# Graph-attention sums of a two-layer GNN kernel: three single-pass products in place of full-precision products

## Chip, cores and metric

The kernel runs on one core of one Trainium2 chip, in one launch. The metric is the device time of that launch in microseconds (us). Engines are named as in the profile: PE (TensorE matmuls), PEld (its weight loads), DVE (VectorE), ACT (ScalarE), POOL (GpSimd), SP (SyncE, which here only issues DMAs).

## Reference

x has 1250 nodes with 1024 features, and there are 41250 edges. Cut to what matters (normalisation and the first layer are only named):

```
edge_index = jnp.stack([src, dst])
h = jnp.maximum(_layernorm(x), 0.0)
x = x + first_layer(h, ...)              # relational convolution, ELU, product with wo; residual h
h = jnp.maximum(_layernorm(x), 0.0)
# second layer: graph attention
h = h @ W                                # 1024 x 1024
al, ar = h @ a_l, h @ a_r
e = exp(-leaky_relu(al[src] + ar[dst], negative_slope=0.1))
rowsum = segment_sum(e, src, num_segments=N)
h_prime = segment_sum(e[:, None] * h[dst], src, num_segments=N)
x = x + elu(h_prime / (rowsum[:, None] + 1e-5))
```

The last segment sum is done densely: the weight of a pair of nodes is (number of edges between them) times e, and h_prime is the 1250 x 1250 weight matrix times h. All of it is float32.

## The kernel before

The 1250 nodes are T = 10 row tiles of 128 (the last has 98 rows). The program goes through four stages.

1. To about 190 us: edges are counted into `cnt` by one-hot products, and the first layer's three products with the weights are made (L720, float32).
2. To about 300 us: `means` (L791) multiplies the counts with y in three bfloat16 parts, `way_back` (L837, L838) multiplies with wo, `add_back` (L843) adds the result to the tile of x, which stays in on-chip memory to the end. The matmul at L838 is the only one in the single-pass 4-byte type `F32R`.
3. From 300 to about 439 us: h @ W. Tiles 0 and 1 are made by `product`. The other eight are made in pairs of tiles, each pair in two units (i, j) of seven half-size products (`p1` to `p7`, all through `seventh`, L946). ACT copies products out of PSUM, DVE adds others to them. `by_dst` (L1006) adds the counts of the two edge types and has a DMA transpose them. `scores` and `row` spread the attention scores for use by `weights`. The order inside this stage is left to the scheduler.
4. From 439 us to the end: for each row tile s, `weights(s)` makes the 128 x 1280 weights (L1017 score sums, L1019 leaky ReLU, L1021 masking by counts, L1022 exponential, L1023 times counts), and `sums(s)` multiplies them with all ten tiles of h (L1070): ten times three matmuls of 342 columns in float32. A column of ones in h gives the row sum. `finish` does the division, the ELU and the residual: DVE at L1034 and L1040, ACT at L1035 and L1038, POOL at L1039 (adds the tile of x), then one DMA of the tile to the output. The last tile goes through `finish_last` in three narrower blocks. weights(s+1) is made while the products of s run.

`long_tile`, `new_h`, `turned` and the `yh`, `x`, `w` tags are the places in on-chip memory which tiles share one after another. Inside `tc.manual_schedule` PE, DVE and ACT keep the order in which the program is written; each engine runs its own instructions in order everywhere.

Of the kernel before, what the change touches and what calls it, by code (L numbers as in the profile page):

```python
# [410 lines left out]
def fast_arm(tc, ctx, edges, firsts, w_root, conv_bias, wo, w_gat, a_gat, out,  # L411
             ident, eps5, eps6, lnw, const, wt, wcat, bias, xs, cnt_raw,
# [8 lines left out]
    FB = [(0, 128), (128, 256)]  # L421
    cnt = cnt_raw.rearrange("p (h r n) -> p h r n", h=T, r=2)
# [15 lines left out]
    def norm_relu(work, xt, n):  # L438
# [11 lines left out]
        h = work.tile([128, D], F32, name="h")  # L450
# [20 lines left out]
    with ExitStack() as c1:  # L471
        hot = c1.enter_context(tc.tile_pool(name="hot", bufs=5))

        room = [yh.tile([128, F + 3 * (F + 2)], F32, name=f"room{t}", tag=f"yh{t}") for t in (9, 8, 7)]
# [113 lines left out]
        def first_part(t):  # L588
# [3 lines left out]
            y = yh.tile([128, F + 3 * (F + 2)], F32, name=f"y{t}", tag=f"yh{t}")  # L592
# [141 lines left out]

    def long_tile(name):
        return work.tile([128, T * 128], F32, name=name, tag="z", bufs=2)
# [8 lines left out]
    rest_w = work.tile([128, D], F32, name="rest_w", tag="h")  # L745
# [22 lines left out]
    wo4 = work.tile([128, D], F32R, name="wo4")  # L768
# [72 lines left out]
    def add_back(t, po):  # L841
        n = ROWS[t]
        nc.vector.tensor_add(xs[t][:n], xs[t][:n], po[:n].rearrange("p a b -> p (a b)"))  # L843

# [12 lines left out]
    def new_h(t):  # L857
        hg = yh.tile([128, D + 2], F32, name=f"h{t}", tag=f"yh{t}")
        hs[t] = hg
        return hg.rearrange("p (h c) -> p h c", h=2)  # L860

    def scores(t):

        n = ROWS[t]
        ends = hs[t].rearrange("p (h c) -> p h c", h=2)[:n, :, H]
        nc.vector.tensor_copy(score[:n, :, t], ends)
        nc.gpsimd.memset(hs[t][:n, H:H + 1], 1.0)
# [17 lines left out]
    slots = [cnt[:, s, 0, :D + 2].bitcast(F32) for s in range(T)] + [meta[:, :H + 1], meta[:, H + 1:D + 2]]  # L885
    t1s, t2s, t4s = slots[0:4], slots[4:8], slots[8:12]
# [46 lines left out]
    def rest_of_pair(i):  # L933
# [3 lines left out]
        p["s4"] = s4  # L937
# [65 lines left out]
    def by_dst(s):  # L1003

        tot = cnt[:, s, 0, :]
        nc.vector.tensor_tensor(tot, tot, cnt[:, s, 1, :], ALU.add)  # L1006
        nc.sync.dma_start_transpose(cnt[:, s, 1, :].rearrange("p (t n) -> p t n", t=T), tot)

    zs = {}

    def weights(s, t0, t1):

        if s not in zs:
            zs[s] = long_tile("z").rearrange("p (t n) -> p t n", t=T)
        c = cnt[:, s, 1, :].rearrange("p (t n) -> p t n", t=T)[:, t0:t1]
        z = zs[s][:, t0:t1, :]
        nc.vector.tensor_tensor(z, rows[:, s:s + 1, :].to_broadcast([128, t1 - t0, 128]),  # L1017
                                n_ar[:, t0:t1, None].to_broadcast([128, t1 - t0, 128]), ALU.add)
        nc.vector.scalar_tensor_tensor(z, z, 0.1, z, op0=ALU.mult, op1=ALU.min)  # L1019

        nc.vector.scalar_tensor_tensor(z, c, 1e30, z, op0=ALU.mult, op1=ALU.min)  # L1021
        nc.scalar.activation(z, z, AF.Exp)  # L1022
        nc.vector.tensor_mul(z, c, z)  # L1023

    def finish(s, inv, parts):

        n = ROWS[s]
        low, high = wt[s % 2], wt[2 + s % 2]
        for p, c0, c1 in parts:
            shape = dict(a=p.shape[1]) if len(p.shape) == 3 else None  # L1030
            lo, hi = low[:n, c0:c1], high[:n, c0:c1]
            if shape:
                lo, hi = (v.rearrange("p (a b) -> p a b", **shape) for v in (lo, hi))
            nc.vector.tensor_scalar(lo, p, inv[:n], 0.0, op0=ALU.mult, op1=ALU.min)  # L1034
            nc.scalar.activation(hi, p, AF.Relu, scale=inv[:n])  # L1035
        lo, hi = low[:n, :D + 1], high[:n, :D + 1]
        low, high = (v[:n].rearrange("p (h c) -> p h c", h=2)[:, :, :H] for v in (low, high))
        nc.scalar.activation(lo, lo, AF.Exp)  # L1038
        nc.gpsimd.tensor_add(high, high, xs[s][:n].rearrange("p (h c) -> p h c", h=2))  # L1039
        nc.vector.scalar_tensor_tensor(lo, lo, -1.0, hi, op0=ALU.add, op1=ALU.add)  # L1040
        nc.sync.dma_start(out[s * 128:s * 128 + n, :].rearrange("p (h c) -> p h c", h=2), low)

    def finish_last(s, inv, p, h0, h1, c0, c1):

        n = ROWS[s]
        lo, hi, x = (w[:n].rearrange("p (h c) -> p h c", h=2)[:, h0:h1, c0:c1]
                     for w in (wt[s % 2], wt[2 + s % 2], xs[s]))
        nc.vector.tensor_scalar(hi, p, inv[:n], 0.0, op0=ALU.mult, op1=ALU.max)
        nc.scalar.activation(lo, p, AF.Exp, scale=inv[:n])
        nc.vector.tensor_add(hi, hi, x)  # L1050
        nc.vector.scalar_tensor_tensor(lo, lo, 1.0, hi, op0=ALU.min, op1=ALU.add)
        nc.sync.dma_start(out[s * 128:s * 128 + n, :].rearrange("p (h c) -> p h c", h=2)[:, h0:h1, c0:c1], lo)

    def sums(s):
        n = ROWS[s]
        z = zs.pop(s)

        def inverse(rowsum):
            inv = small("inv")
            nc.vector.tensor_scalar_add(inv[:n], rowsum, 1e-5)  # L1060
            nc.vector.reciprocal(inv[:n], inv[:n])
            return inv

        if s < T - 1:
            pp, p3 = three("p3")
            for t in range(T):
                for i, (c0, c1) in enumerate(CUTS):
                    c1 = min(c1, D + 1)
                    o = pp[:n, i, :c1 - c0] if i < 2 else p3[:n, :c1 - c0]
                    nc.tensor.matmul(o, z[:ROWS[t], t, :n], hs[t][:ROWS[t], c0:c1], start=(t == 0),  # L1070
                                     stop=(t == T - 1))
            finish(s, inverse(pp[:n, 1, H - 342:H - 341]), [(pp[:n, :, :342], 0, 684), (p3[:n, :341], 684, D + 1)])
        else:

            nc.gpsimd.tensor_scalar_add(xs[s][:n], xs[s][:n], -1.0)
            QH = 448
            for i, (h0, h1, c0, c1) in enumerate([(1, 2, 0, QH), (0, 1, 0, QH), (0, 2, QH, H)]):
                p = bank("p3").rearrange("p a b -> p (a b)")
                o = p[:n, :QH + 1] if i == 0 else p[:n, :(h1 - h0) * (c1 - c0)]
                for t in range(T):  # L1080
                    h = hs[t][:ROWS[t]]
                    cols = h[:, H:H + 1 + QH] if i == 0 else h.rearrange("p (h c) -> p h c", h=2)[:, h0:h1, c0:c1]
                    nc.tensor.matmul(o, z[:ROWS[t], t, :n], cols, start=(t == 0), stop=(t == T - 1))  # L1083
                if i == 0:
                    inv = inverse(o[:, 0:1])
                    o = o[:, 1:]
                finish_last(s, inv, o.rearrange("p (h c) -> p h c", h=h1 - h0), h0, h1, c0, c1)
# [43 lines left out]
    with tc.issue_after(copied[T - 1]):  # L1131
        for s in range(T):
            by_dst(s)
# [5 lines left out]
    s12 = work.tile([128, 2, KH, 128], F32, name="s12", tag="wo4")  # L1139
# [186 lines left out]
```

## Time and profile before

| | us |
|---|---|
| median of 3 runs (620.19 to 620.54) | 620.24 |
| the profiled execution's own time | 620.34 |
| span of the profile, first to last instruction | 618.4 |
| PE busy | 607.4 (98%) |
| DVE busy | 379.6 (61%) |
| ACT busy | 191.0 (31%) |
| POOL busy | 45.1 (7%) |
| granted TensorE clock, mean | 0.996 |

The last stage takes 438.8 to 618.4 us of the span; in 438.8 to 611.0 us PE is busy without a gap, DVE for 100.75 us, ACT for 33.05 us and POOL for 23.47 us. In the lines of the profile L is the line of the kernel, "out<-in" names tiles, "128x512" is partitions times elements. In a timeline a line gives the start, the duration, the engine, the line and the tiles of one instruction (or of several alike, "x4"), and in brackets how long the engine sat idle before it and for what.

### The profile page before, as it was taken

To read this page: it belongs to the slowest core of one execution; us is meant where nothing else is said; L and a number is where in the kernel's file an instruction comes from. 1 tells how busy PE (TensorE), PEld (TensorE's weight loads), DVE (VectorE), ACT (ScalarE), POOL (GpSimd) and SP (SyncE) were. 2 spreads that over 40 slices of the span, in tenths; PEclk is the share of its full clock that TensorE was granted. 3 is DMA by queue.
4 is the path that set the end of the run, shared out by engine and by line. 5 is a ranking of instruction groups with operands and counts; after the bars stand their busy time and mean duration, and the time that the engine had idled before them with its cause. 6 is when DMAs were issued, how large, how long until landed. Compare 5 with 4: busy or idle time off the path is not lost.

```text
span 618.4 us, 7877 instructions
## 1 busy us (share of the span) xinstructions
PE 607.4 (98%) x2828; PEld 416.7 (67%) x2828; DVE 379.6 (61%) x899; ACT 191.0 (31%) x385; POOL 45.1 (7%) x56
## 2 busy tenths in 40 slices
PE   8999999999999999999999999999999999999995
PEld 5566666666657776777667888888666666666652
DVE  5889887787754846679974131233555555666632
ACT  3766556666532000014311223131112211222210
POOL 5010000000000000000000000010011101111110
PEclk9999999999999999999999999999999999999998
DMA  8950111111019200000470000000000000000001
GB/s 281 352 110 16 21 34 36 34 36 27 2 53 318 71 2 1 1 1 1 76 137 1 0 2 0 1 0 1 2 0 35 34 34 36 34 35 34 34 37 31
DMA packets 23688, 30.26 MB, mean 49 GB/s; under 512 B 14550, under 2 KB 14874, under 8 KB 23638
## 3 DMA queue, kind: packets, MB, share of 16 engines
q1 hardware_dynamic: 22070, 24.53, 12.7%
q0 software_dynamic: 1424, 5.12, 4.4%
q8 instruction: 24, 0.39, 0.3%
q14 instruction: 26, 0.21, 0.1%
q10 hardware_dynamic: 144, 0.00, 0.0%
HBM read 16.13 MB, written 5.12 MB: 34 GB/s over the span
## 4 chain that ended last, share of the span: by engine, by line
PE 95%; DMA 2%; SPq 1%; DVE 0%; ACT 0%; issue 0%
PE mm L720 18%; PE mm L1070 17%; PE mm L946 11%; PE mm L791 11%; PE p L1070 8%; PE acc L520 7%; PE mm L837 6%; PE z L946 4%; PE mm L875 3%; PE p L1083 3%; DMA w<-in_w_cat_dram 2%; PE p L875 1%; PE tp L575 1%; PE mm L838 1%; PE tp L910 1%; PE tp L926 1%
## 5 line engine op out<-in xcount | busy, mean ns | idle before, releaser
L720 PE MATMUL mm<-w,hT 128*128 128x429 f32 (+1 forms) x320 | 143.7, 535 | 1.4 <-DMA w<-in_w_cat_dram 1.4
L1070 PE MATMUL mm<-h,z 128*128 128x342 f32 (+1 forms) x360 | 118.5, 450 | 0.0
L519 DVE TENSOR_SCALAR key<-meta 125x320 bf16<-125x320 f16 x330 | 85.5, 301 | 24.2 <-PE acc L520 12.0
L1070 PEld LDWEIGHTS mm<-h,z 128*128 128x128 f32 (+1 forms) x360 | 68.4, 190 | 34.9
L791 PE MATMUL mm<-y,cnt 128*128 128x286 bf16 (+3 forms) x600 | 74.9, 284 | 0.2 <-DVE y L613 0.2
L520 PEld LDWEIGHTS <-lo 125*128 125x128 bf16 x330 | 40.5, 126 | 50.4 <-issue 37.2
L520 PE MATMUL acc<-key,lo 125*128 125x320 bf16 x330 | 72.2, 303 | 0.0
L527 ACT ACTIVATE cnt<-acc 128x320 f32 x110 | 49.9, 454 | 69.9 <-PE acc L520 61.4
L791 PEld LDWEIGHTS <-cnt 128*128 128x128 f16 (+1 forms) x600 | 59.3, 99 | 14.4 <-issue 0.8
L1070 PE MATMUL p<-h,z 128*128 128x341 f32 (+1 forms) x180 | 66.1, 449 | 0.0
L720 PEld LDWEIGHTS mm<-w,hT 128*128 128x128 f32 (+1 forms) x320 | 51.4, 191 | 6.7 <-issue 5.1
L1070 PEld LDWEIGHTS p<-h,z 128*128 128x128 f32 (+1 forms) x180 | 33.7, 188 | 17.7
L946 PE MATMUL mm<-w,a 128*128 128x257 f32 (+3 forms) x192 | 44.8, 380 | 0.0
L946 PEld LDWEIGHTS mm<-w,a 128*128 128x128 f32 (+1 forms) x192 | 35.6, 187 | 6.0 <-ACT h L972 0.4
L837 PE MATMUL mm<-wo,meta 128*128 128x512 f32 (+1 forms) x80 | 37.6, 592 | 0.0
L1039 POOL TENSOR_TENSOR w<-w,x 128x1024 f32<-128x1024 f32 x9 | 23.4, 2597 | 135.3 <-ACT w L1035 135.3
L1019 DVE SCALAR_TENSOR_TENSOR z<-z 128x1280 f32<-128x1280 f32 (+2 forms) x11 | 31.2, 2846 | 0.3
L1022 ACT ACTIVATE z<-z 128x1280 f32<-128x1280 f32 (+2 forms) x11 | 12.9, 1173 | 58.8 <-DVE z L1021 58.8
L1060 DVE TENSOR_SCALAR inv<-mm 128x1 f32<-128x1 f32 x9 | 1.4, 159 | 47.6 <-PE mm L1070 47.6
L1035 ACT ACTIVATE w<-mm,inv 128x684 f32<-128x684 f32 x9 | 7.5, 833 | 74.3 <-DVE w L1034 74.3
L494 DVE TENSOR_TENSOR lo<-meta 125x768 bf16<-125x768 f16 x55 | 30.3, 552 | 0.1
L802 ACT ACTIVATE bias<-bias 128x286 f32<-128x286 f32 (+1 forms) x10 | 4.4, 443 | 79.9 <-DVE bias L801 79.9
(161 smaller groups left out, 727.8 us busy)
## 6 DMA issues: line engine op xcount, KB each, us to landing
x<-h POOLq DMA_DIRECT2D x9, 512.0 KB, 4.6
out_dram<-w SPq DMA_DIRECT2D x9, 512.0 KB, 3.0
x<-in_x_dram SPq DMA_DIRECT2D x8, 512.0 KB, 11.4
w<-in_L_gnn_W_dram SPq DMA_DIRECT2D x8, 512.0 KB, 5.3
w<-in_w_cat_dram SPq DMA_DIRECT2D x8, 429.0 KB, 8.9
a<-in_L_gnn_a_dram SPq DMA_DIRECT2D x2, 512.0 KB, 5.2
wo<-in_L_gnn_wo_weight_dram SPq DMA_DIRECT2D x2, 512.0 KB, 10.4
x<-in_x_dram SPq DMA_DIRECT2D x2, 256.0 KB, 3.0
```

The costliest lines, as they stand in the source:

```text
L494: nc.vector.tensor_tensor(los[q // 2], iota_lo, lows[:, q:q + 2, :].rearrange("p q j -> p (q j)")[:, None, :].to_broadcast([PE_, 128, 2 * J]),
L519: nc.vector.tensor_scalar(key, iota_key, keys[:, q, j:j + 1], None, op0=ALU.is_equal)
L520: nc.tensor.matmul(acc[:, :2 * T * W], los[q // 2][:, :, (q % 2) * J + j], key, start=(j == 0), stop=(j == J - 1))
L527: nc.scalar.activation(cnt_w[:, :, bass.ds(b, W)], a3, AF.Copy)
L720: nc.tensor.matmul(pys[t][:ROWS[t], r, :F + HF], hTs[t][0][:, k, :ROWS[t]], wcat[k][:, r, :], start=(k == 0), stop=(k == KD - 1))
L791: nc.tensor.matmul(pm[:n, r, :f], cnt[:k, h, r, t * 128:t * 128 + n], ybs[h][:k, s, r, :f], start=(h == 0 and s == 0), stop=(h == T - 1 an ...
L837: nc.tensor.matmul(po[:n, c, :], oT[:, i, :n], wo_of[i][:, cs], start=(i == 0), stop=False)
L875: nc.tensor.matmul(o, hT[:, k, :n], wg[k][:, c0:c1], start=(k == 0), stop=(k == KD - 1))
L946: nc.tensor.matmul(o[:a.shape[2], :c1 - c0], a[:, k, :], b[k][:, c0:c1], start=(start and k == 0), stop=(k == KH - 1), skip_group_check=no ...
L1019: nc.vector.scalar_tensor_tensor(z, z, 0.1, z, op0=ALU.mult, op1=ALU.min)
L1039: nc.gpsimd.tensor_add(high, high, xs[s][:n].rearrange("p (h c) -> p h c", h=2))
L1070: nc.tensor.matmul(o, z[:ROWS[t], t, :n], hs[t][:ROWS[t], c0:c1], start=(t == 0), stop=(t == T - 1))
```

## The change

Stage 4 is rewritten; stage 3 gets new work beside it; stages 1 and 2 keep their instructions, except that each tile of x is also stored to DRAM after `add_back`.

[...]
- A row tile s is made in two blocks (s, c) of 512 columns, ten times three matmuls each.
- The leaky ReLU becomes an ACT product by 0.1 (`take_tenth`) and a DVE minimum (`leaky`); one operation (`times_counts`) takes the place of the mask and the product. For s of 2 and more these lie in pieces of 512, 512 and 256 columns (`raw`).
- The row sum comes from four POOL additions (`sum_weights`) and a one-column matmul (`sum_rows`).
- x is stored to DRAM (`xd`) and loaded again block by block (`load_rest`); POOL subtracts 1 from it and adds it (`elu_parts`), DVE makes the last step and SP sends a block of 512 columns out (`put_out`).
- Tiles move: h, hh and the third forms take the places of x, of the weights W and others; the transposed counts and the sums of W lie in the `yh` places.
- The weights of s = 0 and 1 for the first eight tiles are made during the last pair of stage 3; the rest of stage 4 is under `manual_schedule` for PE, DVE and ACT (POOL and SP are left to the scheduler).

The core of the diff (bookkeeping of pools and tags is left out):

```diff
+    dram = ctx.enter_context(tc.tile_pool(name="dram", bufs=1, space=bass.MemoryType.DRAM))
+    xd = [dram.tile([128, D], F32, name=f"xd{t}") for t in range(T)]
...
+        nc.sync.dma_start(xd[t][:n], xs[t][:n])
...
-        hg = yh.tile([128, D + 2], F32, name=f"h{t}", tag=f"yh{t}")
+        hg = big.tile([128, D + 2], F32, name=f"h{t}", tag=f"x{t + 1}") if t % 2 == 0 else long_tile("h")[:, :D + 2]
...
-        nc.gpsimd.memset(hs[t][:n, H:H + 1], 1.0)
...
+    CUT = 1.0 - 2.0 ** -13
+    HD = D // 2
+    hhs, parts = {}, []
+    def low(t):
+        return parts[0][:, t * D:t * D + D]
+    def parts_of(t):
+        n = ROWS[t]
+        h = hs.pop(t).rearrange("p (h c) -> p h c", h=2)[:n, :, :H]
+        if t not in hhs:
+            hhs[t] = big.tile([128, D + 2], F32R, name=f"hh{t}", tag=f"x{t}")
+        hh, hl = (v[:n].rearrange("p (h c) -> p h c", h=2) for v in (hhs[t][:, :D], low(t)))
+        nc.scalar.activation(hh, h, AF.Copy, scale=CUT / 4096.0)
+        nc.vector.scalar_tensor_tensor(hl, hh.bitcast(F32), -4096.0, h, op0=ALU.mult, op1=ALU.add)
...
-    slots = [cnt[:, s, 0, :D + 2].bitcast(F32) for s in range(T)] + [meta[:, :H + 1], meta[:, H + 1:D + 2]]
-    t1s, t2s, t4s = slots[0:4], slots[4:8], slots[8:12]
+    by_dsts, slots, t1s, t2s, t4s = [], [], [], [], []
+    def new_places():
+        for s in range(T):
+            v = yh.tile([128, YW], F32, name=f"d{s}", tag=f"yh{s}")
+            by_dsts.append(v[:, :T * 64].bitcast(F16))
+            slots.append(v[:, T * 64:])
+        slots.extend([meta[:, :H + 1], meta[:, H + 1:D + 2]])
+        t1s.extend(slots[0:4])
+        t2s.extend(slots[4:8])
+        t4s.extend(slots[8:12])
...
-        nc.sync.dma_start_transpose(cnt[:, s, 1, :].rearrange("p (t n) -> p t n", t=T), tot)
+        nc.sync.dma_start_transpose(by_dsts[s].rearrange("p (t n) -> p t n", t=T), tot)
...
-    def weights(s, t0, t1):
...
-    def finish(s, inv, parts):
...
-    def sums(s):
...
+    def raw(s):
+        if s < 2:
+            return [place(early[0]), place(slots[s][:, :256], 8)]
+        return [place(slots[0][:, :HD]), place(slots[1][:, :HD], 4), place(slots[2][:, :256], 8)]
...
+    def add_scores(s, a=0, b=T):
+        for t0, t1, (z,) in each(a, b, raw(s)):
+            nc.vector.tensor_tensor(z, rows[:, s:s + 1, :].to_broadcast([128, t1 - t0, 128]),
+                                    n_ar[:, t0:t1, None].to_broadcast([128, t1 - t0, 128]), ALU.add)
+    def take_tenth(s, a=0, b=T):
+        for t0, t1, (z, y) in each(a, b, raw(s), tenth(s)):
+            nc.scalar.activation(y, z, AF.Copy, scale=0.1)
+    def leaky(s, a=0, b=T):
+        for t0, t1, (z, y) in each(a, b, raw(s), tenth(s)):
+            nc.vector.tensor_tensor(z, z, y, ALU.min)
+    def exps(s, a=0, b=T):
+        for t0, t1, (z,) in each(a, b, raw(s)):
+            nc.scalar.activation(z, z, AF.Exp)
+    def times_counts(s, a=0, b=T):
+        for t0, t1, (z, c) in each(a, b, raw(s), [(0, T, by_dsts[s].rearrange("p (t n) -> p t n", t=T))]):
+            nc.vector.scalar_tensor_tensor(z, z, 3e38, c, op0=ALU.min, op1=ALU.mult)
+    def sum_weights(s, first=True, rest=True):
+        z, y = raw(s), by_dsts[s].bitcast(F32).rearrange("p (t n) -> p t n", n=128)
+        add = nc.gpsimd.tensor_add
+        if first:
+            add(y[:, :4], *((at(z, 0, 4), at(z, 4, 8)) if s < 2 else (z[0][2], z[1][2])))
+            add(y[:, :2], y[:, :2], y[:, 2:4])
+        if rest:
+            add(y[:, :2], y[:, :2], at(z, 8, 10))
+            add(zsum[s % 2], y[:, 0], y[:, 1])
+    def high_parts(s, a=0, b=T):
+        for t0, t1, (z, h) in each(a, b, raw(s), sets[s % 2]["h"]):
+            nc.scalar.activation(h, z, AF.Copy, scale=CUT)
+    def low_parts(s, a=0, b=T):
+        for t0, t1, (z, h, l) in each(a, b, raw(s), sets[s % 2]["h"], sets[s % 2]["l"]):
+            nc.vector.tensor_tensor(l, z, h.bitcast(F32), ALU.subtract)
+    def differences(s, a=0, b=T):
+        for t0, t1, (h, l, m) in each(a, b, *(sets[s % 2][i] for i in "hlm")):
+            nc.vector.scalar_tensor_tensor(m, l.bitcast(F32), -4096.0, h.bitcast(F32), op0=ALU.mult, op1=ALU.add)
+    def third_form(engine, t):
+        n = ROWS[t]
+        engine.tensor_tensor(hms[t][:n, :D], low(t)[:n].bitcast(F32), hhs[t][:n, :D].bitcast(F32), ALU.subtract)
+    sums_of = {}
+    def open_block(s, c, banks=None):
+        if banks is None:
+            p = ps.tile([128, 2, 512], F32, name="mm")
+            banks = p[:, 0, :], p[:, 1, :]
+        sums_of[s, c] = banks
+    def load_rest(s, c):
+        n, x = ROWS[s], buffers(s, c)[2]
+        nc.sync.dma_start(x[:n], xd[s][:n, c * HD:c * HD + HD])
+    def multiply(s, c, forms, a=0, b=T):
+        n, banks = ROWS[s], sums_of[s, c]
+        for t in range(a, b):
+            k = ROWS[t]
+            for f in forms:
+                h = low(t) if f == "l" else (hhs if f == "h" else hms)[t]
+                nc.tensor.matmul(banks[f == "m"][:n], at(sets[s % 2][f], t, t + 1)[:k, 0, :n],
+                                 h[:k, c * HD:c * HD + HD], start=(t == 0 and f in "hm"),
+                                 stop=(t == T - 1 and f in "lm"), skip_group_check=True)
...
+    def sum_rows(s):
+        rowsums[s] = own_bank("rowsum")
+        nc.tensor.matmul(rowsums[s][:ROWS[s], 0, 0:1], zsum[s % 2][:, :ROWS[s]], one, start=True, stop=True)
...
+    def inverse(s):
+        n = ROWS[s]
+        invs[s] = inv = small("inv")
+        nc.vector.tensor_scalar_add(inv[:n], rowsums.pop(s)[:n, 0, 0:1], 1e-5)
+        nc.vector.reciprocal(inv[:n], inv[:n])
...
+    def first_sum(s, c):
+        n = ROWS[s]
+        nc.scalar.activation(buffers(s, c)[0][:n], sums_of[s, c][0][:n], AF.Copy, scale=4097.0)
+    def join(s, c):
+        n = ROWS[s]
+        r = buffers(s, c)[0][:n]
+        nc.vector.tensor_add(r, r, sums_of.pop((s, c))[1][:n])
+    def elu_parts(s, c, quick=False):
+        n = ROWS[s]
+        r, e, x = (v[:n] for v in buffers(s, c))
+        nc.gpsimd.tensor_scalar_add(x, x, -1.0)
+        nc.scalar.activation(e, r, AF.Exp, scale=invs[s][:n])
+        if quick:
+            nc.vector.tensor_scalar(r, r, invs[s][:n], 0.0, op0=ALU.mult, op1=ALU.max)
+            nc.vector.tensor_add(r, r, x)
+        else:
+            nc.scalar.activation(r, r, AF.Relu, scale=invs[s][:n])
+            nc.gpsimd.tensor_add(r, r, x)
+    def put_out(s, c):
+        n = ROWS[s]
+        r, e, x = (v[:n] for v in buffers(s, c))
+        nc.vector.scalar_tensor_tensor(e, e, 1.0, r, op0=ALU.min, op1=ALU.add)
+        nc.sync.dma_start(out[s * 128:s * 128 + n, c * HD:c * HD + HD], e)
...
+    for t in range(2):
+        parts_of(t)
...
-            for t in (2 * i, 2 * i + 1):
-                scores(t)
-            for t in range(0 if i == 1 else 2 * i, 2 * i + 2):
-                row(t)
-            if i == T // 2 - 2:
-                weights(0, 0, T - 2)
-    weights(0, T - 2, T)
-    weights(1, 0, T)
-    for s in range(T):
-        if s >= 1 and s + 1 < T:
-            weights(s + 1, 0, T)
-        sums(s)
+            if after:
+                for t in (2 * i, 2 * i + 1):
+                    scores(t)
+                    parts_of(t)
+                for t in range(0 if i == 1 else 2 * i, 2 * i + 2):
+                    row(t)
+                early += [big.tile([128, D + 2], F32, name="early", tag="x8")[:, :D], long_tile("early")[:, :D]]
+                for s in range(2):
+                    add_scores(s, 0, T - 2)
+                    take_tenth(s, 0, T - 2)
+                    leaky(s, 0, T - 2)
+                    exps(s, 0, T - 2)
+                    times_counts(s, 0, T - 2)
+                    sum_weights(s, rest=False)
+                    if s == 0:
+                        high_parts(s, 0, T - 2)
+                        low_parts(s, 0, T - 2)
+    ends = [slots[i][:, :HD] for i in range(5, 9)] + [meta[:, i * HD:i * HD + HD] for i in range(2)]
+    hms = {k: big.tile([128, D + 2], F32R, name=f"hm{k}", tag=f"w{k}") for k in range(T - 2)}
+    A, B = T - 2, T
+        for t in range(4):
+            third_form(nc.gpsimd, t)
+        for c in range(2):
+            open_block(0, c)
+            load_rest(0, c)
+        multiply(0, 0, "hl", 0, A)
+        for t in (A, A + 1):
+            scores(t)
+        hhs[A] = work.tile([128, KD * 128], F32R, name="hh8", tag="hT", bufs=2)
+        parts_of(A)
+        hhs[A + 1] = big.tile([128, D + 2], F32R, name="hh9", tag="x9")
+        parts_of(A + 1)
+        sets[1]["h"], sets[1]["l"] = [place(wide("zh", "wo4"))], [place(wide("zl", "h"))]
+        high_parts(1, 0, A)
+        low_parts(1, 0, A)
+        for t in (A, A + 1):
+            row(t)
+        multiply(0, 1, "hl", 0, A)
+        for s in range(2):
+            add_scores(s, A, B)
+            take_tenth(s, A, B)
+        for s in range(2):
+            leaky(s, A, B)
+            exps(s, A, B)
+        for s in range(2):
+            times_counts(s, A, B)
+            sum_weights(s, first=False)
+            high_parts(s, A, B)
+        for i in (1, 0):
+            sets[i]["m"] = [place(work.tile([128, T * 128], F32R, name="zm", tag="z", bufs=2))]
+        for s in range(2):
+            low_parts(s, A, B)
+        hms[A] = work.tile([128, KD * 128], F32R, name="hm8", tag="hT", bufs=2)
+        hms[A + 1] = big.tile([128, D + 2], F32R, name="hm9", tag="x8")
+        differences(0)
+        for t in range(4, T):
+            third_form(nc.vector, t)
+        pair = [bank("tp").rearrange("p a b -> p (a b)") for _ in range(2)]
+        open_block(1, 0, pair)
+        multiply(1, 0, "hl", 0, A)
+        for s, c in ((0, 0), (0, 1), (1, 0)):
+            multiply(s, c, "hl", A, B)
+        first_sum(0, 0)
+        multiply(0, 0, "m")
+        sum_rows(0)
+        for s in range(T):
+            if s:
+                if s + 1 < T:
+                    high_parts(s + 1)
+                if s > 1:
+                    open_block(s, 0)
+                join(s - 1, 1)
+                elu_parts(s - 1, 1)
+                if s + 1 < T:
+                    low_parts(s + 1)
+                    differences(s + 1)
+                put_out(s - 1, 1)
+            if s + 2 < T:
+                add_scores(s + 2)
+                take_tenth(s + 2)
+            if s:
+                load_rest(s, 0)
+                if s > 1:
+                    multiply(s, 0, "hl")
+                first_sum(s, 0)
+                multiply(s, 0, "m")
+                sum_rows(s)
+                open_block(s, 1)
+                load_rest(s, 1)
+                multiply(s, 1, "hl")
+            else:
+                differences(1)
+            join(s, 0)
+            inverse(s)
+            elu_parts(s, 0)
+            if s + 2 < T:
+                leaky(s + 2)
+                exps(s + 2)
+            put_out(s, 0)
+            if s + 2 < T:
+                times_counts(s + 2)
+                sum_weights(s + 2)
+            first_sum(s, 1)
+            multiply(s, 1, "m")
+        join(T - 1, 1)
+        elu_parts(T - 1, 1, quick=True)
+        put_out(T - 1, 1)
```

## The prediction

> **What bounds the kernel now.** I read the page first (busy shares, slices), then the stretches by stage, then the timelines of DVE and POOL over one row tile of the last stage, and last the chain of waits for the pace of each kind of matmul.
>
> ```profile
> PE 607.4 (98%) x2828; PEld 416.7 (67%) x2828; DVE 379.6 (61%) x899; ACT 191.0 (31%) x385; POOL 45.1 (7%) x56
> ...
> PE   8999999999999999999999999999999999999995
> ...
> DVE  5889887787754846679974131233555555666632
> ...
> POOL 5010000000000000000000000010011101111110
> PEclk9999999999999999999999999999999999999998
> ```
> ```profile
> 338.80:411.00 72.20, 72.08 (x355) 62.08 (x355) 15.41 (x39) 17.85 (x34) 3.16 (x5) 1.00 0.00 1
> 411.00:438.80 27.80, 27.76 (x131) 22.68 (x130) 10.04 (x19) 5.99 (x12) 0.29 (x3) 1.00 0.00 1
> 438.80:611.00 172.20, 172.20 (x601) 110.62 (x599) 100.75 (x97) 33.05 (x39) 23.47 (x10) 1.00 0.08 29
> ```
>
> PE is the bound everywhere, without a gap from 438.8 us on. So a gain must come from PE time, and it lasts only until another engine is full. DVE has 71 us left in the last stage.
>
> The DVE and POOL timelines of one row tile (start, duration) show one tile and the start of the next, 17.25 us later (524.20 - 506.95):
>
> ```profile
> 506.95 0.16 DVE L1060 TENSOR_SCALAR inv<-mm 128x1 f32<-128x1 f32 x1 [5.07 <-PE mm L1070]
> ...
> 508.67 1.48 DVE L1017 TENSOR_TENSOR z<-meta,score 128x1280 f32<-128x1280 f32 x1
> 510.19 3.52 DVE L1019 SCALAR_TENSOR_TENSOR z<-z 128x1280 f32<-128x1280 f32 x1
> 513.64 1.22 DVE L1040 SCALAR_TENSOR_TENSOR w<-w,w 128x1025 f32<-128x1025 f32 x1
> 514.77 1.48 DVE L1021 SCALAR_TENSOR_TENSOR z<-cnt,z 128x1280 f32<-128x1280 f16 x1
> ...
> 524.20 0.16 DVE L1060 TENSOR_SCALAR inv<-mm 128x1 f32<-128x1 f32 x1 [5.07 <-PE mm L1070]
> ```
> ```profile
> 407.06 2.77 POOL L1075 TENSOR_SCALAR x<-x 98x1024 f32<-98x1024 f32 x1 [16.38 <-ACT h L451]
> ...
> 509.74 2.62 POOL L1039 TENSOR_TENSOR w<-w,x 128x1024 f32<-128x1024 f32 x1 [14.63 <-ACT w L1035]
> ...
> 596.00 2.34 POOL L1039 TENSOR_TENSOR w<-w,x 128x1024 f32<-128x1024 f32 x1 [14.63 <-ACT w L1035]
> ```
>
> L1019 and L1021 have the same shape, yet L1019 takes 3.52 us and L1021 1.48. L1019 is the one under which POOL works: POOL's addition runs to 512.36, and 512.36 plus one undisturbed 1.35 is 513.71, where L1019 ends. DVE stood still until POOL was done. In turn POOL's addition takes 2.62 where it starts under L1017, and 2.34 at 596.00 where DVE rests. [...] Today that costs DVE 2 us per tile, hidden behind PE.
>
> For the pace of matmuls, the chain of waits:
>
> ```profile
> 209.25 1.72 PE mm L837 x4
> ...
> 211.20 1.72 PE mm L837 x4
> ...
> 335.24 0.87 PE z L946 x4
> ```
>
> Between the two L837 groups lie 1.95 us; 1.72 of it is float32, so the `F32R` matmul of 512 columns (L838) costs 0.23. Float32 halves of 256 columns step at 0.87/4 = 0.216, each with its own 0.19 us weight load hidden. I take 0.22 for an `F32R` matmul with its load.
>
> **PE.** Removed: 17.25 us per tile. Added: 60 x 0.22 = 13.2. If PE stayed the bound, ten tiles would gain 40 us.
>
> **DVE, per row tile.** Two-input operations step at (duration less 0.08) 0.6 us for 512 columns, 0.33 for 256, 1.13 for 1024 (513.64 to 514.77), 1.5 for 1280. `add_scores`, `leaky`, `times_counts` and `low_parts` are each 512 + 512 + 256 = 1.53; `differences` 1.5; two `put_out` 1.2. That is 8.8 us on two on-chip inputs. Two `join`, with one input in PSUM, 1.2; `inverse` 0.4. Sum 10.4: less than PE's 13.2.
>
> **POOL, per row tile.** From 2.34 for 1024 columns, and some start-up per instruction (0.1 to 0.2, my estimate): 1.25 for 512, 0.7 for 256, 0.45 for 128. `sum_weights` is 1.25 + 0.7 + 0.7 + 0.45 = 3.1; two additions of x 2.5. The two subtractions of 1: 1024 columns took 2.77 (L1075), 110 columns 0.75 (L642), so 0.5 + 2.2 per 1000: 1.64 each for 512. POOL has 8.9 us per tile, where it had 2.6.
>
> Does the subtraction, with one input, exclude DVE too? The trace is silent: three of 110 columns at 12.83 to 15.19 leave DVE's two-input L646 at 0.30, but they hardly stream. [...]
>
> **The period of the new loop.** DVE and POOL obey a fixed order. Iteration s on DVE: `join`(s-1,1), `low_parts`(s+1), `differences`(s+1), `put_out`(s-1,1), `add_scores`(s+2), `join`(s,0), `inverse`, `leaky`(s+2), `put_out`(s,0), `times_counts`(s+2). `put_out`(s-1,1) waits for POOL's addition, and in POOL's queue, as the program's order of instructions has it, `sum_weights`(s+1) with a subtraction in its middle stands before that addition. So first comes what excludes each other: POOL 3.1 + 1.64 + 1.25, DVE 1.53 + 1.5, together 9.0, or 7.5 if about 1.5 us of POOL's start-up holds nothing. Then a chain: `put_out` 0.6, `add_scores` 1.53, last piece of `take_tenth` on ACT 0.5, `first_sum`(s,0) 0.6, queued behind it on ACT, `join` 0.65, `inverse` 0.4, ACT's exponential and ReLU 1.1, rest of a `leaky` piece 0.3, POOL's addition 1.25, `put_out` 0.6, `times_counts` 1.53: 9.06. The period is 16.6 to 18.1; I take 17.3. It was 17.25. DVE's and POOL's order takes PE's place, and PE idles about 4 us per tile.
>
> SP's queue: `load_rest`(s,1) can go out only when POOL's addition (s-1,1) has freed its place. A 256 KB load took 3.0 us to land; with 0.2 to issue and the 1.64 subtraction that is 4.8 us until POOL can add (s,0), against 5.4 in the chain above: covered, by 0.6. The ten stores of x go out in stage 2, where DMA is mostly idle, and the next readers come tens of us later: nothing. In SP's queue nine of them stand before the transposes of `by_dst`, one behind; `parts` lies on `cnt`, so DVE's first `parts_of` waits for the transposes, 0 to 1 us in a stretch where PE has 13.8 us of `product` to do: nothing.
>
> **The way in.** Let T0 = 438.8 be the end of the pair products. After it PE has `hl` products to do (13.2 us), but DVE must first finish tiles 8 and 9: ACT and the last addition 1.7; two-input work 7.5 (two `parts_of` and `low_parts`(1) at 1.13, eight pieces of 256 at 0.33, `differences`(0) 1.5); score rows 0.6; ACT's part in the chain 1.9; held by POOL: the rest of four `third_form` of 2.34 each, 3.65, and `sum_weights` 2.3. That is 17.7. Then six `third_form` on DVE 6.8 (PE's third product waits for each), `add_scores`(2) 1.5, `differences`(1) 1.5, `join` and `inverse` 1.05, `leaky` 1.5, addition 1.25, `put_out` and `times_counts` 2.1: iteration 1 begins 33.4 us after T0.
>
> **The way out.** Iterations 1 to 7 take 7P. From the start of iteration 8: 9.7 to `put_out`(7,1), `join`(8,0) 10.3, the load and subtraction for (8,1) 13.9, addition, `put_out`(8,0) 15.8, `join`(8,1) 16.4; only that frees PSUM for block (9,1). PE takes block (9,0) until 18.6 (6.6, and 1.7 for a lowered clock, below), (9,1) until 25.2; `join` to `put_out` 3.3; from the last DVE instruction to the end 6.3, as before (612.1 to 618.4). Sum 34.8.
>
> **The clock.** The row shows 9 throughout, as PE never rests. [...]
>
> **Stage 3.** Added: eight `parts_of` (ACT 1.06, DVE 1.13) and the weights of s = 0, 1. DVE has 75 us to spare there (338.8 to 438.8), ACT 76, so by sum nothing; but a copy that queues behind one 1.06 us ACT operation (0.39 + 1.06) nearly uses up the 1.73 us that one product gives. Between 0 and 6 us; I take 2.5.
>
> **Sum.** Before, T0 to the end is 618.4 - 438.8 = 179.6. After: 2.5 + 33.4 + 7P + 34.8 = 70.7 + 7P; at P = 17.3 it is 191.8, so 12.2 more. The profiled execution took 620.34, its span 618.4; the median is 620.24, so the sum moves to it unchanged: 632.4.
>
> **Rivals.**
> - *Faster: POOL and DVE do not hold each other up* (L1019's 3.52 would have another cause). Then POOL's 6.0 us run beside DVE; P is 6.0 + 9.06 - 0.3 = 14.8, the way in loses the 5.95 that POOL held and is 27.4, the way out loses 3.0 (9.0 to 6.0) and is 31.8: 2.5 + 27.4 + 31.8 + 103.6 = 165.3, 14.3 less than before: 606. Even so PE's 40 us are not reached, since the chain stays in DVE's order. It decides from P = 15.6 downward (70.7 + 7P = 179.6). Against it: L1019 shows the stall in eight tiles, and POOL's two lengths. For it: POOL's small operations may hold DVE less. Chance 0.13.
> - *Only the subtraction holds nothing*: 1.64 of DVE's work moves under POOL's, so 6.2 to 7.4 in place of 7.5 to 9.0; P 15.3 to 16.5, 618 to 627, mostly 622. Chance 0.17.
> - *Slower than my sum: single-pass matmuls do not keep 0.22 with a new weight load each.* At 0.30 PE needs 18 us per tile, 180 for ten, and the way in comes on top: about 645. L946's 0.216 with loads of 0.19 speaks against it. With it I count POOL dearer than estimated and stage 3 disturbed: 640 to 660. Chance 0.15.
> - The change not doing what it says has no room: `F32R` is in the trace.
>
> **How the numbers follow.** My forecast, P 16.6 to 18.1, gives 627 to 638 (70.7 + 7P at both ends), chance 0.55. The range 612 to 645 leaves out most of the first rival and half of the third, about 0.18. No change that can be told means within 0.2%, 1.2 us: 0.04, from the second rival. Faster: 0.13 and 0.05 of the second, 0.18; slower 0.78.
>
> **What would show it.** After: PE with gaps of 3 to 6 us in the last stage, waiting for DVE's `join`; the granted clock there below 0.95; row tiles 16.6 to 18.1 us apart; two-input DVE operations of 512 columns at well over 0.7 us wherever POOL adds; `F32R` matmuls stepping at 0.22; a stretch of some 10 us of idle PE after the pair products; DVE and POOL together nearly full. Tiles 13 to 15 us apart, or PE full to the end, would make the prediction wrong.

## The result, and the profile after

The changed kernel takes 668.95 us (668.13 to 670.32, 4 runs), the kernel before 620.39 us beside it: ratio 1.0783, 95% interval 1.0764 to 1.0803. The prediction had 632.4 us and a range of 612 to 645. The direction came out as forecast, but the loss is 48.6 us where the forecast had 12.2, and the time lies above the range.

The page of the changed kernel, its busy shares and some rows of its slices:

```profile
PE 600.8 (90%) x2848; PEld 430.4 (64%) x2848; DVE 416.9 (62%) x1000; ACT 249.4 (37%) x497; POOL 130.1 (19%) x119
...
PE   7999999999999999999999999985659677967993
...
DVE  5888888887638464989534132759764547545511
...
POOL 4100000000000000000000000192554255434530
PEclk9999999999999999999999999998878889878997
```

In the last stage (from slice 28 on) no engine is full: PE, DVE and POOL all rest, and the clock row falls from 9 to 7 and 8 in places. A stage in which nobody is full is ruled by waits. The stretches of that stage (busy time of each engine, then granted clock, DMA share and GB/s) are the end of the pair products, the way in, iterations 1 to 7 of the loop, and the way out:

```profile
411.00:440.40 29.40, 28.88 (x138) 23.58 (x137) 15.98 (x23) 12.25 (x18) 8.61 (x6) 1.00 0.05 16
440.40:472.00 31.60, 20.19 (x76) 14.26 (x75) 28.11 (x37) 11.75 (x21) 17.27 (x11) 0.86 0.04 13
472.00:623.40 151.40, 113.74 (x414) 87.59 (x414) 86.39 (x134) 58.14 (x106) 69.65 (x57) 0.86 0.14 49
623.40:668.40 45.00, 31.22 (x133) 22.38 (x131) 12.27 (x20) 9.57 (x15) 15.76 (x12) 0.92 0.14 48
```

The prediction had 441.3 for the end of the pair products (440.4 came), 33.4 for the way in (31.6), 121.1 for seven tiles (151.4) and 34.8 for the way out (45.0). Two terms of the sum carry the whole miss: 30.3 and 10.2 us. Within the loop the mean tile takes 21.6 us in place of 17.3.

The waits of the changed kernel from 470 us on (engine and line, whom it waited for, us in total, times, longest) name the cause:

```profile
DVE d L1175 <- PE mm L1149: 62.2, 17, 5.9
...
PE mm L1149 <- ACT d L1170: 46.8, 18, 6.4
...
ACT d L1089 <- DVE d L1084: 33.1, 9, 4.7
```

L1175 is `join`, L1149 `multiply`, L1170 `first_sum`, L1089 `take_tenth`, L1084 `add_scores`. Each factor of the sums has a high part, a low part and a third form, the difference of the two: `multiply` gathers high x high and low x low (the first product of a block) in one PSUM bank and third x third (the third product) in another, ACT copies the first out scaled by 4097 (`first_sum`), and DVE adds the third (`join`). The prediction had PE wait for DVE's `join`. It is the other way round: `join` waits for PE, and PE in turn waits for ACT's copy `first_sum`, 18 times, a wait that stands nowhere in the prediction. The timeline of one row tile shows the chain (the first line is the third product of the block before it):

```profile
534.04 2.61 PE L1149 MATMUL mm<-hm,zm 128*128 128x512 f32 x10 [0.75 <-ACT d L1170]
...
542.35 0.69 DVE L1193 SCALAR_TENSOR_TENSOR meta<-meta,d 128x512 f32<-128x512 f32 x1 [1.15 <-POOL d L1188]
542.96 1.62 DVE L1084 TENSOR_TENSOR d<-meta,score 128x512 f32<-128x512 f32 x3
...
543.67 1.54 ACT L1089 ACTIVATE d<-d 128x512 f32<-128x512 f32 x3 [4.71 <-DVE d L1084]
545.12 0.58 ACT L1170 ACTIVATE d<-mm 128x512 f32<-128x512 f32 x1
...
545.75 4.63 PE L1149 MATMUL mm<-hm,zm 128*128 128x512 f32 x10 [4.47 <-ACT d L1170]
...
550.18 0.42 PE L1157 MATMUL rowsum<-one,bias 128*128 128x1 f32 x2
...
550.49 0.69 DVE L1175 TENSOR_TENSOR d<-d,mm 128x512 f32<-128x512 f32 x1 [5.91 <-PE mm L1149]
```

Read it backwards. `join` starts at 550.49, when the ten matmuls of the third product (hm, zm) end. They start at 545.75, 0.05 us after the copy of the first product has ended, although their inputs had been there since `differences` of the iteration before. They write the second bank of the PSUM tile `mm` of which ACT reads the first (PSUM is the memory into which PE writes its products; a tile here is two banks of 512 columns). The copy itself stood on ACT behind `take_tenth`, which stands behind `add_scores`, which stands behind `put_out`. After the 4.47 us of rest the ten matmuls take 4.63 us (4.14 in every other tile); those of the block before, ten alike, take 2.61 at 534.04. The run that keeps PE busy, below, ties this to the rest.

The kernel holds its own counter-example. Block (1, 0) is opened on two separate PSUM banks (`tp`). The timeline of the changed kernel around it:

```profile
474.05 2.49 PE L1149 MATMUL tp<-hm,zm 128*128 128x512 f32 x10
...
482.77 0.58 ACT L1170 ACTIVATE d<-tp 128x512 f32<-128x512 f32 x1
483.38 0.69 DVE L1175 TENSOR_TENSOR d<-d,tp 128x512 f32<-128x512 f32 x1 [0.97 <-ACT d L1170]
```

Here the third product was done 6 us before its copy began, and `join` follows the copy by 0.03 us, where in the tile above it follows it by 4.79 (550.49 less 545.70). From the first addition of `sum_weights` (L1109) in iteration 0 to that in iteration 1, 471.75 to 489.21, are 17.46 us, close to the forecast's 17.3. Every later iteration uses the pair tile, and takes about 22.3 (six of them from 489.21 to 623.14).

### The profile page after: what moved, and what is told of

It is laid out like the page before. It is cut to its first block, busy times and chain, and to the rows that moved or that the text cites. A ratio compares the mean times of both kernels' runs of the same rounds, so it can differ in the third digit from the quotient of the medians.

```text
span 668.4 us, 8320 instructions
## 1 busy us (share of the span) xinstructions
PE 600.8 (90%) x2848; PEld 430.4 (64%) x2848; DVE 416.9 (62%) x1000; ACT 249.4 (37%) x497; POOL 130.1 (19%) x119
## 3 DMA queue, kind: packets, MB, share of 16 engines
HBM read 21.25 MB, written 10.24 MB: 47 GB/s over the span
## 4 chain that ended last, share of the span: by engine, by line
PE 75%; DVE 11%; ACT 4%; issue 4%; POOL 2%; DMA 2%; SPq 1%; ACTq 0%; DVEq 0%; POOLq 0%
PE mm L721 15%; PE mm L1149 14%; PE mm L985 11%; PE mm L797 10%; PE acc L521 6%; PE mm L843 5%; PE z L985 4%; PE mm L901 3%; DMA w<-in_w_cat_dram 2%; DVE parts L1121 2%; DVE d L1084 2%; DVE zm L1125 2%; ACT d L1170 1%; PE p L901 1%; PE tp L576 1%
## 5 line engine op out<-in xcount | busy, mean ns | idle before, releaser
L1149 PE MATMUL mm<-hm,zm 128*128 128x512 f32 (+3 forms) x190 | 65.3, 498 | 50.1 <-ACT d L1170 46.8
L1149 PEld LDWEIGHTS mm<-hm,zm 128*128 128x128 f32 (+3 forms) x190 | 43.6, 238 | 70.0 <-ACT d L1170 54.3
L1175 DVE TENSOR_TENSOR d<-d,mm 128x512 f32<-128x512 f32 (+1 forms) x19 | 13.1, 688 | 65.9 <-PE mm L1149 62.2
L1109 POOL TENSOR_TENSOR d<-early 128x512 f32<-128x512 f32 x2 | 2.6, 1282 | 239.8 <-PE mm L985 233.8
L985 PE MATMUL mm<-w,a 128*128 128x257 f32 (+3 forms) x192 | 44.8, 380 | 0.5 <-ACT h L1000 0.5
L1149 PE MATMUL mm<-hh,parts 128*128 128x512 f32 x100 | 41.7, 417 | 0.0
L1149 PE MATMUL mm<-parts 128*128 128x512 f32 x100 | 40.7, 407 | 0.2 <-DVE parts L1121 0.2
L1149 PE MATMUL mm<-hh,zh 128*128 128x512 f32 (+1 forms) x90 | 35.9, 399 | 0.0
L1149 PE MATMUL mm<-parts,zl 128*128 128x512 f32 (+1 forms) x90 | 35.4, 393 | 0.0
L1089 ACT ACTIVATE d<-d 128x512 f32<-128x512 f32 (+1 forms) x26 | 13.5, 546 | 45.3 <-DVE d L1084 45.0
```

What stands on the lines that cost most here:

```text
L985: nc.tensor.matmul(o[:a.shape[2], :c1 - c0], a[:, k, :], b[k][:, c0:c1], start=(start and k == 0), stop=(k == KH - 1), skip_group_check=no ...
L1089: nc.scalar.activation(y, z, AF.Copy, scale=0.1)
L1149: nc.tensor.matmul(banks[f == "m"][:n], at(sets[s % 2][f], t, t + 1)[:k, 0, :n], h[:k, c * HD:c * HD + HD], start=(t == 0 and f in "hm"), ...
```

## The experiments

The edits shift the line numbers by one or two, which is why `join` is L1175, L1176 or L1177. For each kernel the table has the median, the ratio to the kernel before with its interval, the mean period of seven tiles (first to eighth addition that opens `sum_weights`, divided by 7) and the way out (from 0.25 us after the eighth of them to the end of the span).

| kernel | us | ratio | tile | way out |
|---|---|---|---|---|
| as changed | 668.95 | 1.0783 (1.0764 to 1.0803) | 21.63 | 45.0 |
| third product in a bank of its own | 628.84 | 1.0140 (1.0123 to 1.0157) | 17.05 | 36.0 |
| copy ahead of `take_tenth` | 632.92 | 1.0205 (1.0188 to 1.0222) | 16.37 | 44.7 |
| PE kept busy | 662.91 | 1.0684 (1.0667 to 1.0702) | 19.76 | 51.1 |
| no row sums | 658.60 | 1.0612 (1.0593 to 1.0631) | see below | see below |
| first two together | 620.75 | 1.0002 (0.9992 to 1.0012) | 15.95 | 36.3 |
| ... and subtraction folded away | 608.21 | 0.9803 (0.9787 to 0.9820) | 14.85 | 31.2 |
| ... and additions of x on VectorE | 603.29 | 0.9723 (0.9707 to 0.9740) | 13.66 | 33.8 |
| fold alone | 660.94 | 1.0643 (1.0625 to 1.0661) | 20.61 | 44.8 |

**A bank of its own for the third product.**

```diff
     def open_block(s, c, banks=None):
...
-            p = ps.tile([128, 2, 512], F32, name="mm")
-            banks = p[:, 0, :], p[:, 1, :]
-        sums_of[s, c] = banks
+            banks = ps.tile([128, 2, 512], F32, name="mm")[:, 0, :]
+        sums_of[s, c] = [banks, None]
     def multiply(s, c, forms, a=0, b=T):
         n, banks = ROWS[s], sums_of[s, c]
+        if "m" in forms:
+            banks[1] = bank("third").rearrange("p a b -> p (a b)")
...
```

> Edit: the third product of a block gets a PSUM bank of its own in place of the second bank of the pair that holds the first product. Theory A (in the changed kernel the third product waits for ACT's scaled copy of the first, because both lie in one PSUM tile; the copy stands on ACT behind take_tenth, PE idles, and ten matmuls at a lowered clock then lie between copy and join: 4.8 us per row tile that the forecast did not count): the third product runs right behind the others, join waits for the copy alone, row tiles fall from 22 to about 17 us, and with about 6 us in the way out the time falls from 669 to 620-632. Theory B (GpSimd and VectorE excluding each other cost 14 us per tile where the forecast had 9): the wait only changes its name, 660-669.

It took 628.84 us, 40 less. The timeline of this kernel, one tile:

```profile
512.95 2.49 PE L1150 MATMUL third<-hm,zm 128*128 128x512 f32 x10
...
514.46 1.54 ACT L1089 ACTIVATE d<-d 128x512 f32<-128x512 f32 x3 [6.77 <-DVE d L1084]
515.90 0.58 ACT L1171 ACTIVATE d<-mm 128x512 f32<-128x512 f32 x1
...
516.51 0.69 DVE L1176 TENSOR_TENSOR d<-d,third 128x512 f32<-128x512 f32 x1 [1.15 <-ACT d L1171]
```

The third product runs ahead of the copy at full pace, and `join` is released by the copy. This is the chain that the prediction had written down, and its sum comes out with it: 17.05 us per tile against 17.3, 36.0 for the way out against 34.8. The two parts of the period fit as well: from the start of `sum_weights` to `put_out` 7.8 us (522.39 to 530.20) where the forecast had 7.5 to 9.0, and 9.2 from there to the next `sum_weights` where it had 9.06. The rival, that POOL and DVE hold each other for 14 us per tile, falls.

**The copy ahead of `take_tenth`.** The PSUM tiles stay as they were.

```diff
                 add_scores(s + 2)
-                take_tenth(s + 2)
+                if not s:
+                    take_tenth(s + 2)
...
                 first_sum(s, 0)
+                if s + 2 < T:
+                    take_tenth(s + 2)
                 multiply(s, 0, "m")
```

> Edit: on ACT, take_tenth(s+2) stands behind first_sum(s,0) in place of ahead of it; the PSUM tiles stay as they are. Theory A: the copy can run when the first product ends, some 5 us earlier, and the third product runs under add_scores; row tiles about 16.5-17 us, the way out (which has no take_tenth) and the wait of the second block as they were: 628-636. Theory B: 660-669.

632.92 us. The wait of PE for the copy is still there, but it ends early and lies under DVE's work: `join` waits 0.15 us for PE where it waited 5.91.

```profile
528.24 0.60 ACT L1170 ACTIVATE d<-mm 128x512 f32<-128x512 f32 x1 [2.42 <-PE mm L1149]
...
528.89 2.60 PE L1149 MATMUL mm<-hm,zm 128*128 128x512 f32 x10 [0.75 <-ACT d L1170]
...
531.60 0.69 DVE L1175 TENSOR_TENSOR d<-d,mm 128x512 f32<-128x512 f32 x1 [0.15 <-PE mm L1149]
```

The way out has no `take_tenth` and stays at 44.7. So the two things that made the wait long, the shared tile and the place of the copy, are each enough to take most of it away.

**PE kept busy.** It separates the wait from the lowered clock.

```diff
                 first_sum(s, 0)
+                idle = own_bank("idle").rearrange("p a b -> p (a b)")
+                for t in range(18):
+                    nc.tensor.matmul(idle, at(sets[s % 2]["h"], 0, 1)[:, 0, :], hhs[t % 8][:, :HD], start=True, stop=True)
                 multiply(s, 0, "m")
```

> Edit: 18 single-pass matmuls of 512 columns, whose product nobody reads, fill most of PE's idle time ahead of the third product of each first block (s of 1 to 9). Theory A: only the clock's part goes, ten matmuls in 2.6 in place of 4.6 us: 2 us per row tile in nine tiles, 649-655. A rival inside A, that those matmuls are slow for another reason than the clock (reads of the same PSUM tile, or weights): no gain, 667-675. Theory B: no gain, 667-671.

662.91 us: less gained than expected, for a reason of place. In the loop the timeline shows

```profile
537.07 4.36 PE L1370 MATMUL idle<-hh,parts 128*128 128x512 f32 x18
541.74 2.59 PE L1149 MATMUL mm<-hm,zm 128*128 128x512 f32 x10 [0.31 <-ACT d L1170]
```

with 2.59 in place of 4.63, and the granted clock of its loop (493 to 611 us) is 1.00, where the changed kernel's was 0.88. The tile falls by 1.87 us, seven times that is 13.1 us. So the slow matmuls are a matter of PE's rest before them, not of PSUM or weights. But in tiles 8 and 9 PE has little idle time: the third product starts 3.3 us after its copy has ended there (617.62 to 620.95), and the way out grows by 6 us. I had counted those two tiles as a gain.

**No row sums.**

```diff
     def sum_weights(s, first=True, rest=True):
-        z, y = raw(s), by_dsts[s].bitcast(F32).rearrange("p (t n) -> p t n", n=128)
-        add = nc.gpsimd.tensor_add
-        if first:
...
+        if s < 2 and not rest:
+            nc.gpsimd.memset(zsum[s], 8.0)
```

> Edit: GpSimd's additions of the weights over the tiles of sources (sum_weights) are left out, a constant stands for the row sums. This takes 3.1 of GpSimd's 8.9 us per tile. Theory A: the stretch in which the two engines hold each other shortens by at most 2 us per tile and the wait for the third product stays: 650-660. Theory B: a third of 14 us per tile goes, 4.6 us in seven tiles and 2 in the way in: 633-640.

This kernel leaves the row sums out, so it does not compute the layer; it only shows what they cost. 658.60 us. By the starts of `add_scores` in iterations 2 to 7 the tile takes 20.78 us in place of 22.26, so 3.1 us of POOL work are worth 1.5 while the wait stands.

**The fold alone.** POOL's subtraction of 1 from x goes into an addition that DVE makes in stage 2; the layer norm in between takes off the mean.

```diff
     def add_back(t, po):
...
-        nc.vector.tensor_add(xs[t][:n], xs[t][:n], po[:n].rearrange("p a b -> p (a b)"))
+        nc.vector.scalar_tensor_tensor(xs[t][:n], xs[t][:n], -1.0, po[:n].rearrange("p a b -> p (a b)"),
+                                       op0=ALU.add, op1=ALU.add)
...
     def elu_parts(s, c, quick=False):
-        nc.gpsimd.tensor_scalar_add(x, x, -1.0)
```

> Edit: only the subtraction of 1 leaves GpSimd (folded into the addition of the second stage); the third product still waits for ACT's copy. Theory A: with the wait in place, the two subtractions (1.5 us each) count for what put_out waits for GpSimd, 1.15 and 1.4 us, so at most 1.2 us per tile and some 3 us in the way out: 656-664. If each subtraction held VectorE for its whole length as the forecast's rule had it, the tile would lose 2.5-3 us: 645-650.

660.94 us, 1.0 us per tile. It is no 2.5 to 3 us: the forecast's period counts 1.64 us for a subtraction among what excludes each other, but the two subtractions of a tile do not hold DVE for their length. The way out stays at 44.8, where some 3 us less were expected.

**Both edits of the wait.**

> Edit: the two edits together (a bank of its own for the third product, and take_tenth behind the copy). Theory A: what is left is the forecast's chain without its ACT link; in the run with own banks 1.15 us lie between the last add_scores and join, which now go, so row tiles come 15.7-16.2 us apart in place of 17.06, and the time is 619-623. A rival: join is then held by something else that was hidden (the copy waits for PE's next block), and nothing is gained over the run with own banks, 627-630.

620.75 us, the time of the kernel before within a tenth of a per cent. ACT's link is gone from the chain and 1.1 us with it.

**Both, and the fold.**

> Edit: both edits, and the subtraction of 1 from x leaves GpSimd: it is folded into the addition that makes x in the second stage (a VectorE instruction that exists already), since the layer norm that reads x in between takes its mean off anyway. Theory A: GpSimd has 3 us less per tile, of which put_out(s-1,1) waits for 1.5-2.5; row tiles 13.4-14.5 us apart, near PE's 13.3 of work, time 602-612, under the kernel before. Rival: DMA now holds the addition (load_rest takes 3 us and has nothing behind it to hide), row tiles above 15, 615-622.

608.21 us: 1.1 us per tile (14.85, a little above the 13.4 to 14.5 expected), and 5 us in the way out, where each block waits for load, subtraction and addition in turn.

**The additions of x on VectorE as well.** This came out of the timeline of the run before:

```profile
534.59 1.63 DVE L1126 SCALAR_TENSOR_TENSOR zm<-parts 128x1280 fp32r<-128x1280 f32 x1
534.83 2.54 POOL L1189 TENSOR_TENSOR d<-d,meta 128x512 f32<-128x512 f32 x1
...
537.40 0.69 DVE L1194 SCALAR_TENSOR_TENSOR meta<-meta,d 128x512 f32<-128x512 f32 x1 [1.18 <-POOL d L1189]
```

POOL's addition starts 0.24 us after DVE's `differences`, is held by it, and DVE then waits 1.18 us for it; undisturbed it takes 1.29. On DVE it takes 0.7.

```diff
     def elu_parts(s, c, quick=False):
...
-            nc.gpsimd.tensor_add(r, r, x)
     def put_out(s, c):
...
+        nc.vector.tensor_add(r, r, x)
         nc.vector.scalar_tensor_tensor(e, e, 1.0, r, op0=ALU.min, op1=ALU.add)
```

> Edit: as the run with both edits and the folded subtraction, and GpSimd's additions of x (two per tile) go to VectorE, right ahead of put_out; GpSimd keeps the row sums alone. In the run before, GpSimd's addition held differences and stood 2.5 us on the path, another 1.3 later, with 0.1 of hand-over each; VectorE takes 0.6 for each. Theory A: row tiles 13.6-14.4 us apart in place of 14.85, the way out 1-2 us shorter, 600-604. Rival: VectorE, with 11.6 us of its own and the 3.1 us that the row sums still hold it, is the bound, and nothing is gained, 606-611.

603.29 us, 17 less than the kernel before. The stretches of this kernel, loop and way out, and the way out of the run before:

```profile
470.80:566.50 95.70, 95.70 (x420) 77.85 (x419) 94.54 (x149) 58.20 (x106) 28.66 (x29) 1.00 0.22 78
566.50:600.30 33.80, 23.34 (x103) 17.16 (x101) 15.69 (x24) 9.29 (x15) 3.79 (x4) 0.88 0.18 63
...
575.39:606.58 31.19, 19.57 (x86) 14.07 (x84) 12.86 (x21) 9.09 (x15) 10.18 (x8) 0.89 0.21 68
```

PE is busy for all 95.70 us of the loop at clock 1.00, 13.66 us per tile, which is 60 matmuls at 0.228. The change's saving on PE is there at last, in seven tiles. DVE, at 94.54 of 95.70, is as good as full too. The way out became 2.6 us longer, not shorter: PE no longer runs ahead, so it has 103 matmuls left at that point where it had 86, 3.8 us more, and the last `join` waits for PE.

## Why the prediction was right and wrong

- **The step that failed** is the chain in "The period of the new loop": "`first_sum`(s,0) 0.6, queued behind it on ACT, `join` 0.65". Between the two lies the third product, which waits for the copy because both use one PSUM tile. I had the copy's place in ACT's queue right, and did not ask who besides `join` waits for it. Measured, 4.79 us pass between the end of the copy and `join`. So the term between the copy and `join`, which the chain put at nothing, is 4.8 us: 17.3 and 4.8 are 22.1; the tiles after the first take 22.3. With the shared tile undone the tile takes 17.05.
- **The direction** was no luck: with the wait undone and the rest as it was, the kernel takes 628.84, still 1.4% more than before. As forecast, the order of DVE and POOL takes PE's place in the loop (17.05 us per tile against 17.25 before), and the way in and the way out add the rest.
- **The clock.** The stretches of the changed kernel around the tile above (PE busy, then the granted clock) are

```profile
541.50:544.91 3.41, 0.00 (x0) 1.00 0.37 136
544.91:551.74 6.83, 5.99 (x15) 0.50 0.03 11
551.74:555.15 3.41, 3.41 (x16) 1.00 0.01 2
```

  A stretch of 3.41 us without a matmul is followed by 6.83 us at half clock, in which the ten matmuls come 0.44 us apart (545.75 to 550.18); those of the block before come 0.245 apart (534.04 to 536.49). The forecast's period has no term for this: these ten matmuls were on the path, and the lowered clock cost 1.87 us per tile by the run that keeps PE busy. The 1.7 us for a lowered clock in the forecast's way out is shown by no run: in this kernel the third products there take 2.57 to 2.60, at a granted clock of 1.00 (616.60 to 657.60).
- **The way out** (45.0 against 34.8) is the same step: PE makes each of the last four blocks strictly as two products, a wait for the copy, and the third product, about 8.1 us per block where I had 6.6, and does not run ahead. A bank of its own makes it 36.0.
- **The pace of `F32R`**, a rival at 0.15, was no cause: a matmul takes 0.23 us at full clock, against 0.22.
- **POOL and DVE.** POOL's additions and DVE's operations held each other up, as forecast: in the run with both edits and the fold, `low_parts` takes 3.23 us under `sum_weights` (1.62 in the run without row sums), POOL's addition beside `differences` 2.54 in place of 1.29. (The 1.35 us that the forecast gave an undisturbed L1019 is shown by no run; L1021, of the same shape, takes 1.48.) For the subtraction the forecast counted 1.64 us held, a term that no run shows; what the runs show is far less. In the run with both edits:

```profile
530.46 1.50 POOL L1182 TENSOR_SCALAR meta<-meta 128x512 f32<-128x512 f32 x1 [2.93 <-DMA meta<-xd]
...
530.58 1.64 DVE L1093 TENSOR_TENSOR d<-d,d 128x512 f32<-128x512 f32 x2
```

  The subtraction takes 1.50 with `leaky` running beside it all the while (1.49 in the changed kernel at 545.26, where DVE rests), and `leaky` 1.64 in place of 1.27. So 0.4 us are held, not 1.6; the tile's other subtraction, beside `low_parts`, takes 1.93 in place of 1.50, again 0.4. The rival in which the subtraction holds nothing was the nearer one. It cost the subtraction's 1.1 us per tile all the same, because the addition that `put_out` waits for stands behind it in POOL's queue.
- **The faster rival**, that the two do not hold each other up at all, is excluded by the same lines; the way to a faster kernel was to take POOL's work off the path, not that it ran beside DVE's.
- **The loads of x** cost nothing in the changed kernel, as forecast: POOL waits 25.8 us for them over nine blocks, but its additions afterwards still wait 52.0 us for ACT. An issue took 0.32 us, where the forecast had 0.2.
- **The way in** (31.6 against 33.4) and the shift of stage 3 (1.6 against 2.5) held within 2 us.
- **PE as the bound.** "If PE stayed the bound, ten tiles would gain 40 us": it is the bound in the last kernel, whose seven tiles take 13.66 each in place of 17.25, 25 us less; the rest, mostly the way in and the way out, takes 8 of these back, and 17 are left.

## What to carry to other kernels

For each instruction on a chain ask not only what it waits for but what else waits for it: here a copy out of one bank of a PSUM tile held the next matmuls into the same tile, though they wrote the other bank, and a tile of its own for them, or an earlier place for the copy in its engine's queue, took the wait off the path. A stage that was bound by one full engine, and afterwards by none, has become a ring of waits; read the ring link by link in the timeline of one period before sizing any engine's work.

## What was not expected of the hardware

The lowered clock did not always begin where the rest ended, and it came after rests shorter than one of its steps of 3.41 us. In the run with a bank of its own, PE rests for 2.65 us; the matmuls after it are 0.23 us apart at first, and slow ones come only 1.4 us later:

```profile
533.60 0.50 PE L1150 MATMUL mm<-hh,zh 128*128 128x512 f32 x1 [2.65 <-ACT d L1171]
...
535.38 0.63 PE L1150 MATMUL mm<-hh,zh 128*128 128x512 f32 x1
...
535.81 0.63 PE L1150 MATMUL mm<-parts,zl 128*128 128x512 f32 x1
```

The stretches of the same time (PE busy, then the granted clock):

```profile
531.32:534.74 3.42, 1.14 (x5) 1.00 0.43 155
534.74:538.15 3.41, 3.41 (x10) 0.50 0.00 0
538.15:541.56 3.41, 3.41 (x16) 1.00 0.49 154
```

In the changed kernel the granted clock was 0.50 in eight stretches before PE's last matmul, three of 3.41 us, three of 6.83 and two of 10.24, and they begin (463.00, 483.48, 500.54, 524.43, 544.91, 568.81, 589.29, 613.18) whole multiples of 3.41 us apart. A step before one of them did not have to be idle: half clock followed 459.58 to 463.00 with 1.49 us of PE's work in it, and 480.06 to 483.48 with 1.30; it did not follow 445.93 to 449.34 with 1.70. That the work in a step decides was not shown, as no run varied it alone. In the run with a bank of its own, the step above at half clock costs some 1.5 us: ten matmuls from 534.40 to 538.27 take 3.87 us, where ten at full clock take 2.3.
